# The first 40 microseconds of a two-layer transformer kernel: ScalarE normalisation, later constants, shared low parts, queries before keys

## The chip, the cores and the metric

The kernel is one program on one core of a Trainium2 chip. The metric is device time in microseconds for one launch that does everything: loading, both layers, storing.

The engines are TensorE (PE in the profile, with weight loads as PEld), VectorE (DVE), ScalarE (ACT), GpSimd (POOL) and SyncE (SP). Each runs its own instructions strictly in the order of its queue. DMAs are issued from the queues of SP, ACT and POOL.

## The reference

```python
x = L0_attn_hidden_states                      # (4, 512, 512)
x = x + layernorm(attn0(layernorm(x), Wq, Wkv, Wo))     # layer 0
x = x + layernorm(ffn0(layernorm(x), scales, vals, bias))
x = x + layernorm(attn1(layernorm(x), ...))             # layer 1
x = x + layernorm(ffn1(layernorm(x), ...))

def attn0(h, Wq, Wkv, Wo):                     # 32 query heads of 16, one key/value head of 16
    q = h @ Wq                                 # (4, 512, 512)
    k, v = split(h @ Wkv)                      # (4, 512, 16) each
    s = q . k * 16**-0.5 + alibi               # causal
    return (softmax(s) . v) @ Wo
```

Layer 1 has a low-rank attention with 32 heads of 128 and a ternary feed-forward part. The change touches only the layer-0 attention.

## The kernel before, in words

The work is in three stages that follow each other: `A1`/`A2` (layer 0, with layer 1's weight products mixed in, to about 680 us), `phase_b` (layer 1's attention) and `C` (layer 1's feed-forward part).

All products are made exact enough by splitting each float32 operand into a rounded high part and a low part, the difference (`split`, L66: ScalarE casts the high part at L68, another engine subtracts at L69). One product is then three matmuls: high by high (L160), high by low (L161), low by high (L162), in `mm3_gen`.

`A1.begin` (L543) is the start, and what the change touches:

- `ks_tile(i)` (L286) makes a key tile KS of batch i: a memset and two DMAs of 32 KB issued by GpSimd (L291). `qs_tile(m)` (L294) makes a query tile QS of head group m (8 heads) with two DMAs of 128 KB issued by GpSimd (L298). These constants carry the position bias.
- `load_x0` (L245) issues four DMAs from SP, one for each 128 rows of batch 0 (256 KB each, tile `ot`). `setup` (L259) loads the key weights from ScalarE's queue, and the four 256 KB pieces of the query weights and the mask from SP's. `setup_wq` (L273) splits the query weights in four pieces, with the subtraction on GpSimd.
- `front(b, x)` (L311) normalises the four row blocks of a batch (`ln_gen`, L99: statistics on VectorE, the power -0.5 on GpSimd at L108, the negative mean times scale on VectorE at L112). The normalised rows `xn` are made by ScalarE for batches 1 to 3 (L329) and by VectorE for batch 0 (`ln_apply`, L167). Then each block is transposed by TensorE (L148), its high part cast by ScalarE (L150, `xt_h`), its low part subtracted by VectorE (L152, `xt_l`). After the fourth block `front` projects keys and values (12 matmuls, into `po` for batch 0) and fills KS on ScalarE and VectorE (L352, L354).
- `qproj(b, m)` (L374) projects a group of queries (12 matmuls into `mm`), casts `qh` (L386), subtracts `ql` (L389), and for batch 0 calls `spread` (L400): for each of four pairs, two matmuls with a selection matrix (L409) and two ScalarE copies into QS (L412). Group 0 spreads through PSUM tiles `ps`, the other groups through the two `mm` banks that all projections share (`Tok(2)`).

After `begin`, `run` (L593) goes through 128 units and 13 more to drain. In unit u the row maxima of one column of scores are taken (`max_tile`: matmuls L453 and L457, a reduction on VectorE at L461). Twelve units later the exponentials (L496, L499) and the products with the values (L512) follow. Between these steps `slot` moves every generator in `gens` on by one step: the remaining projections (`projections`, L572), the reloads of queries (`loads`), and from unit 12 the weight products and the later parts of layer 0. Unit 8 m is the first that needs the queries of group m.

Program order is only a priority. `TileContext` orders each engine's queue before the launch, by its own modelled times; `issue_after(ins)` adds the rule that instructions traced in the block stand behind `ins` on the engine of `ins`.

Of the kernel before, what the change touches and what calls it, by code (L numbers as in the profile page):

```python
# [14 lines left out]
AF = mybir.ActivationFunctionType  # L15
# [27 lines left out]
def f(ap):  # L43
    return ap.bitcast(F32)
# [21 lines left out]
def split(nc, h, l, raw, eng):  # L66

    nc.scalar.copy(h, raw)  # L68
    return eng.tensor_tensor(l, raw, f(h), ALU.subtract)  # L69
# [29 lines left out]
def ln_gen(nc, c, pool, src, name="ln_nm"):  # L99

    st = pool.tile([128, 6], F32, name="ln_st", tag="ln_st")
    nc.vector.bn_stats(st, src)
    mv = pool.tile([128, 2], F32, name="ln_mv", tag="ln_mv")
    nc.vector.bn_aggr(mv, st)
    ve = pool.tile([128, 1], F32, name="ln_ve", tag="ln_ve")
    nc.vector.tensor_scalar(ve, mv[:, 1:2], 1e-5, None, ALU.add)
    rs = pool.tile([128, 1], F32, name="ln_rs", tag="ln_rs")
    c.last_pow = nc.gpsimd.tensor_tensor(rs, ve, c.mhalf, ALU.pow)  # L108
    yield from hop(3)
    nm = pool.tile([128, 1], F32, name=name, tag=name,  # L110
                   **({"bufs": 16} if name == "shift" else {}))
    nc.vector.scalar_tensor_tensor(nm, mv[:, 0:1], -1.0, rs, ALU.mult, ALU.mult)  # L112
    return rs, nm
# [31 lines left out]
def transpose_gen(nc, c, bank, src, dst_h, dst_l):  # L145
    ps = yield from bank.take([128, KC, 128])
    for k in range(KC):
        nc.tensor.transpose(ps[:, k, :], src[:, bass.ts(k, 128)], c.ident)  # L148
    yield from hop(1)
    nc.scalar.copy(dst_h, ps)  # L150
    yield from hop(2)
    nc.vector.tensor_tensor(dst_l, ps, f(dst_h), ALU.subtract)  # L152
    bank.give()
    yield from hop(1, 1)


def mm3_gen(nc, ps, lh, ll, rh, rl, ks, hops=2, stop=True):
    n = len(ks)
    for j, k in enumerate(ks):
        nc.tensor.matmul(ps, lh(k), rh(k), start=(j == 0), stop=False)  # L160
        nc.tensor.matmul(ps, lh(k), rl(k), start=False, stop=False)  # L161
        nc.tensor.matmul(ps, ll(k), rh(k), start=False, stop=(stop and j == n - 1))  # L162
        yield from hop(hops)


def ln_apply(nc, dst, src, rs, nm):
    nc.vector.tensor_scalar(dst, src, rs, nm, ALU.mult, ALU.add)  # L167
# [49 lines left out]
class A1:  # L217
# [54 lines left out]

    def setup_wq(self):  # L273
        for k in range(KC):
            last = split(self.nc, self.wq_h[:, k], self.wq_l[:, k], self.raw[:, k], self.nc.gpsimd)
        return last

    def setup_consts(self):
        with self.tc.issue_after(self.c.last_pow.ins):
            for m in range(1, 4):  # L280
                self.qs_tile(m)
            for i in range(1, B):
                self.ks_tile(i)
            self.zero = f(self.KS[B - 1][64:68, 0, :])
# [26 lines left out]
    def front(self, b, x):  # L311

        nc, c = self.nc, self.c
        mmp, tok = self.mmp, self.tok
        if x is None:
            x = {}
            for t in range(2):
                x[t] = self.load_x(b, t)
            yield from hop(8)
        while self.projected < 4 * b:  # L320
            yield
        xt_h = self.xtp.tile([128, KC, S], F32R, name="xt_h", tag="xt_h")
        xt_l = self.xtp.tile([128, KC, S], F32R, name="xt_l", tag="xt_l")
        self.xt = xt_h, xt_l
        for t in range(4):
            rs, nm = yield from ln_gen(nc, c, self.sm, x[t])
            xn = self.tmp.tile([128, D], F32, name="xn", tag="xn", bufs=3)
            if 1 and b > 0:
                nc.scalar.activation(xn, x[t], AF.Identity, bias=nm, scale=rs)  # L329
            else:  # L330
                ln_apply(nc, xn, x[t], rs, nm)
            if t + 2 not in x and t < 2:
                x[t + 2] = self.load_x(b, t + 2)
            yield from hop(2)
            ts = bass.ts(t, 128)
            yield from transpose_gen(nc, c, self.bank, xn, xt_h[:, :, ts], xt_l[:, :, ts])
        self.fronted = b + 1
        spare = b == 0
        if spare:
            ps = self.psO.tile([128, S], F32, name="po", tag="po")  # L340
        else:
            yield from tok.take()
            ps = mmp.tile([128, S], F32, name="mm", tag="mm")
        yield from mm3_gen(nc, ps, lambda k: self.wk_h[:, k], lambda k: self.wk_l[:, k],
                           lambda k: xt_h[:, k], lambda k: xt_l[:, k], range(KC))
        vt = self.qp.tile([32, S], F32, name="vt", tag="ql")
        nc.scalar.copy(vt, ps[32:64])
        yield
        for two in range(2):
            o = 64 * two  # L350
            ks = self.KS[b][:, two]
            nc.scalar.activation(ks[o:o + 48], ps[o:o + 48], AF.Copy, scale=0.25)  # L352
            yield from hop(3)
            nc.vector.scalar_tensor_tensor(  # L354
                ks[o + 32:o + 48], ps[o + 32:o + 48], 0.25, f(ks[o + 32:o + 48]),
                ALU.mult, ALU.subtract)
            yield
        if spare:
            psv = self.psT.tile([128, 4, 32], F32, name="ptv", tag="pt")
        else:  # L360
            tok.give()
            yield from tok.take()
            psv = mmp.tile([128, 4, 32], F32, name="mmv", tag="mm")
        for t in range(4):
            nc.tensor.transpose(psv[:, t], vt[:, bass.ts(t, 128)], c.ident[:32, :32])
        vx = self.vp.tile([128, 4, 32], F32, name="vx", tag="vx")
        nc.gpsimd.memset(vx, 1.0)
        yield
        nc.vector.tensor_copy(vx[:, :, 0:16], psv[:, :, 16:32])
        if not spare:  # L370
            tok.give()
        self.vx[b] = vx
# [170 lines left out]
    def begin(self):  # L543
        self.gens = []
        self.mn = None
        self.pe = {}
        self.tok = Tok(2)
        self.bank = Bank(self.mmp, "mm", self.tok)
        self.KS, self.QS = {}, {}
        self.ks_tile(0)  # L550
        self.qs_tile(0)
        x = self.load_x0()
        self.sel_tile()
        self.setup()
        fr = self.front(0, x)
        while True:
            n = self.c.__dict__.get("last_pow")
            next(fr)
            self.npow = getattr(self, "npow", 0) + (self.c.__dict__.get("last_pow") is not n)
            if self.npow == 4:  # L560
                break
        with self.tc.issue_after(self.c.last_pow.ins):
            last = self.setup_wq()
        with self.tc.issue_after(last.ins if 0 else self.c.last_pow.ins):
            self.setup_consts()
        for _ in fr:
            pass
        for m in range(2):
            for _ in self.qproj(0, m):
                pass  # L570

    def projections(self):  # L572

        for m in range(2, 4):
            yield from self.qproj(0, m)
        for b in range(1, B):
            yield from self.front(b, None)
            for m in range(4):
                yield from self.qproj(b, m)
# [814 lines left out]
```

## Time and profile before

| quantity | value |
|---|---|
| median of 3 runs | 2357.81 us (2349.78, 2357.81, 2358.64) |
| the profiled execution | 2349.14 us |
| its span, first to last instruction | 2347.1 us |
| TensorE busy | 2279.2 us (97%) |
| VectorE busy | 1577.6 us (67%) |
| ScalarE busy | 1069.2 us (46%) |
| GpSimd busy | 1175.6 us (50%) |
| mean granted TensorE clock | 0.999 |

The profiled execution took 2.04 us more than its span, and its time is that of the fastest of the three runs. TensorE is busy nearly everywhere except at the start, so the place to read is the first of the page's 40 slices and, inside it, what each engine waits for. A wait is named as waiter, then what released it.

### The profile page before, as it was taken

To read this page: it belongs to the slowest core of one execution; us is meant where nothing else is said; L and a number is where in the kernel's file an instruction comes from. 1 tells how busy PE (TensorE), PEld (TensorE's weight loads), DVE (VectorE), ACT (ScalarE), POOL (GpSimd) and SP (SyncE) were. 2 spreads that over 40 slices of the span, in tenths; PEclk is the share of its full clock that TensorE was granted. 3 is DMA by queue.
4 is the path that set the end of the run, shared out by engine and by line. 5 is a ranking of instruction groups with operands and counts; after the bars stand their busy time and mean duration, and the time that the engine had idled before them with its cause. 6 is when DMAs were issued, how large, how long until landed. Compare 5 with 4: busy or idle time off the path is not lost.

```text
span 2347.1 us, 35936 instructions
## 1 busy us (share of the span) xinstructions
PE 2279.2 (97%) x11638; PEld 1785.0 (76%) x11638; DVE 1577.6 (67%) x4664; ACT 1069.2 (46%) x2404; POOL 1175.6 (50%) x1390
## 2 busy tenths in 40 slices
PE   5999999999999999999999999999999999999998
PEld 4666566656677888888888888888888888878886
DVE  5755767676467777777777777777677678764443
ACT  4655555354424444444444444444444445443332
POOL 4323443434336656656656656666656657522221
PEclk9999999999999999999999999999999999999999
DMA  3555553534471412422422422412412312051100
GB/s 90 172 158 170 144 145 87 145 87 140 156 220 61 134 65 87 138 68 80 138 70 78 140 68 79 142 65 88 133 65 89 114 59 77 10 157 32 36 23 18
DMA packets 155534, 236.30 MB, mean 101 GB/s; under 512 B 26274, under 2 KB 91042, under 8 KB 146516
## 3 DMA queue, kind: packets, MB, share of 16 engines
q1 hardware_dynamic: 137732, 195.33, 26.8%
q0 software_dynamic: 14768, 35.92, 5.4%
q10 hardware_dynamic: 2848, 2.76, 0.4%
q8 instruction: 93, 1.52, 0.3%
q14 instruction: 93, 0.76, 0.1%
HBM read 180.03 MB, written 61.83 MB: 103 GB/s over the span
## 4 chain that ended last, share of the span: by engine, by line
PE 84%; DMA 4%; issue 4%; DVE 4%; ACT 2%; POOL 2%; SPq 0%; ACTq 0%; POOLq 0%; DVEq 0%
PE mm L183 11%; PE mm L184 10%; PE mm L185 10%; PE pt L978 5%; PE po L512 3%; PE mm L160 3%; PE mm L162 3%; PE mm L161 3%; PE po L992 3%; PE po L993 3%; PE po L991 3%; PE pt L496 3%; PE ps L958 3%; PE gu L1209 3%; PE ps L959 3%
## 5 line engine op out<-in xcount | busy, mean ns | idle before, releaser
L969 POOL TENSOR_TENSOR s<-s,r 128x384 f32<-128x384 f32 (+3 forms) x512 | 360.2, 721 | 122.6 <-DVE r L968 110.1
L966 ACT ACTIVATE s<-s,mn 128x384 f32<-128x384 f32 (+3 forms) x512 | 285.8, 560 | 226.6 <-DVE mn L962 225.0
L852 POOL TENSOR_TENSOR rp_a<-rp_a,rp_b 128x512 f32<-128x512 f32 x155 | 200.5, 1293 | 300.1 <-DVE rp_b L851 298.4
L981 ACT CAST ph<-pt 128x512 fp32r<-128x512 f32 x320 | 183.0, 586 | 306.5 <-PE pt L978 304.7
L461 DVE CUSTOM_DVE_ANT_0 jk<-ps,mask 128x384 bf16<-128x384 f32 (+3 forms) x512 | 227.2, 482 | 64.4 <-PE ps L457 63.3
L962 DVE CUSTOM_DVE_ANT_0 s<-ps,mask 128x384 f32<-128x384 f32 (+2 forms) x384 | 204.0, 552 | 41.0 <-PE ps L960 22.6
L982 DVE TENSOR_TENSOR pl<-pt,ph 128x512 fp32r<-128x512 f32 x320 | 218.1, 685 | 19.5 <-ACT ph L981 15.9
L499 ACT ACTIVATE pe<-pt 128x512 f32<-128x512 f32 x307 | 175.1, 601 | 96.0 <-PE pt L496 84.2
L183 PE MATMUL mm<-xh,w_h 128*128 128x512 f32 x512 | 206.3, 403 | 3.6 <-DVE rp_b L851 3.5
L978 PE MATMUL pt<-ident,s 128*128 128x128 f32 x1280 | 209.1, 272 | 0.3 <-DVE pl L982 0.2
L183 PE MATMUL mm<-w_h,oh 128*128 128x512 f32 x512 | 203.3, 397 | 2.6 <-DVE rp_b L851 1.9
L184 PE MATMUL mm<-xl,w_h 128*128 128x512 f32 x512 | 204.9, 400 | 0.0
L185 PE MATMUL mm<-xh,w_l 128*128 128x512 f32 x512 | 202.0, 395 | 0.0
L184 PE MATMUL mm<-w_l,oh 128*128 128x512 f32 x512 | 200.9, 392 | 0.0
L185 PE MATMUL mm<-w_h,ol 128*128 128x512 f32 x512 | 200.7, 392 | 0.0
L978 PEld LDWEIGHTS pt<-ident,s 128*128 128x128 f32 x1280 | 162.7, 140 | 44.2 <-POOL s L969 0.4
L501 POOL TENSOR_SCALAR_AFFINE_SELECT pe<-pe 128x512 f32<-128x512 f32 x128 | 83.2, 654 | 225.6 <-ACT pe L499 223.9
L854 POOL TENSOR_TENSOR ql<-rp_a,qh 128x512 fp32r<-128x512 f32 x124 | 160.2, 1292 | 20.4 <-ACT qh L853 20.1
L848 DVE TENSOR_TENSOR rp_a<-mm,cosq 128x512 f32<-128x512 f32 x128 | 88.3, 690 | 93.6 <-PE mm L185 84.0
L958 PE MATMUL ps<-k,qh 128*128 128x384 f32 (+2 forms) x384 | 139.1, 362 | 1.0 <-DVE mn L962 1.0
L998 DVE TENSOR_TENSOR ol<-po,oh 128x512 fp32r<-128x512 f32 x128 | 87.7, 685 | 68.9 <-ACT oh L997 68.8
L968 DVE RECIPROCAL r<-l 128x1 f32<-128x1 f32 x512 | 74.6, 157 | 87.8 <-ACT s L966 85.6
(330 smaller groups left out, 5796.8 us busy)
## 6 DMA issues: line engine op xcount, KB each, us to landing
xh<-xt SPq DMA_DIRECT2D x32, 1024.0 KB
xl<-xt SPq DMA_DIRECT2D x32, 1024.0 KB
raw<-in_a_wo SPq DMA_DIRECT2D x32, 256.0 KB
vh<-v SPq DMA_DIRECT2D x32, 256.0 KB
vl<-v SPq DMA_DIRECT2D x32, 256.0 KB
w_h<-in_a_wo POOLq DMA_DIRECT2D x32, 256.0 KB, 3.1
m_d<-t_d SPq DMA_DIRECT2D x192, 42.5 KB
raw<-in_a_wq SPq DMA_DIRECT2D x28, 256.0 KB
```

The lines of the kernel that those rows point to most:

```text
L183: nc.tensor.matmul(ps, lh(k), rh(k), start=(j == 0), stop=False)
L184: nc.tensor.matmul(ps, lh(k), rl(k), start=False, stop=False)
L185: nc.tensor.matmul(ps, ll(k), rh(k), start=False, stop=(j == n - 1))
L461: nc.vector.tensor_tensor_reduce(out=jk[:, :nk], in0=p, in1=self.c.mask[:, 384 - 128 * qb:512], scale=-1.0, scalar=3e38, op0=ALU.add, op1= ...
L852: eng.tensor_tensor(a, a, r, ALU.add)
L958: nc.tensor.matmul(ps[:, :nk], qh[:, qs], k[:, 0, :nk], start=True, stop=False)
L962: nc.vector.tensor_tensor_reduce(out=s[:, :nk], in0=ps[:, :nk], in1=mask, scale=-1.0, scalar=3e38, op0=ALU.add, op1=ALU.min, accum_out=mn)
L966: nc.scalar.activation(s[:, :nk], s[:, :nk], AF.Exp, bias=mn, scale=-1.0, accum_out=l)
L969: nc.gpsimd.tensor_tensor(s[:, :nk], s[:, :nk], r.to_broadcast([128, nk]), ALU.mult)
L978: nc.tensor.transpose(pt[:, j], PS[u, qb, j][:, bass.ts(kb, 128)], c.ident)
L981: nc.scalar.copy(ph, pt)
L982: nc.vector.tensor_tensor(pl, pt, f(ph), ALU.subtract)
```

## The change

Five edits, all at the start of layer 0:

1. `front` makes `xn` on ScalarE (L329) for batch 0 too; VectorE's `ln_apply` is no longer used there.
2. KS0 and QS0, with their four GpSimd DMAs, are made behind the fourth power of batch 0, no longer first of all.
3. `setup_wq` gives the low parts of pieces 0 and 1 to VectorE, those of 2 and 3 stay on GpSimd. The other constants (QS1 to QS3, KS1 to KS3) stand behind the last of these subtractions on GpSimd, before it was behind the fourth power.
4. `front` of batch 0 calls `qproj(0, 0)` ahead of its key and value projection.
5. `qproj(0, 1)` is no longer done in `begin`; it comes first in `projections`, inside `run`.

```diff
 def setup_wq(self):
     for k in range(KC):
-        last = split(self.nc, self.wq_h[:, k], self.wq_l[:, k], self.raw[:, k], self.nc.gpsimd)
+        last = split(self.nc, self.wq_h[:, k], self.wq_l[:, k], self.raw[:, k],
+                     self.nc.vector if k < 2 else self.nc.gpsimd)
     return last
 def setup_consts(self):
-    with self.tc.issue_after(self.c.last_pow.ins):
+    if True:
         for m in range(1, 4):
             self.qs_tile(m)
...
 def front(self, b, x):
...
-        if 1 and b > 0:
-            nc.scalar.activation(xn, x[t], AF.Identity, bias=nm, scale=rs)
-        else:
-            ln_apply(nc, xn, x[t], rs, nm)
+        nc.scalar.activation(xn, x[t], AF.Identity, bias=nm, scale=rs)
...
     spare = b == 0
+    if spare:
+        yield from self.qproj(0, 0)
     if spare:
         ps = self.psO.tile([128, S], F32, name="po", tag="po")
...
 def begin(self):
...
-    self.ks_tile(0)
-    self.qs_tile(0)
     x = self.load_x0()
...
     with self.tc.issue_after(self.c.last_pow.ins):
+        self.ks_tile(0)
+        self.qs_tile(0)
         last = self.setup_wq()
-    with self.tc.issue_after(last.ins if 0 else self.c.last_pow.ins):
+    with self.tc.issue_after(last.ins):
         self.setup_consts()
     for _ in fr:
         pass
-    for m in range(2):
+    for m in range(1, 1):
         for _ in self.qproj(0, m):
             pass
 def projections(self):
-    for m in range(2, 4):
+    for m in range(1, 4):
         yield from self.qproj(0, m)
```

## The prediction

> **What bounds the kernel now.** I read the page's 40 slices first, to find where TensorE is not full. Each digit is the busy share of a slice of 58.7 us in tenths.
>
> ```profile
> PE   5999999999999999999999999999999999999998
> ```
>
> Only the first slice has much to give. So the next view is the table of stretches, cut at what happens there: 23.2 us is the first projection matmul, 37.8 the first score, 66.1 the first exponential. Columns after the stretch: its length, then busy time (and instructions) of PE, PEld, DVE, ACT, POOL, then clock, DMA share, GB/s.
>
> ```profile
> 0.00:23.20 23.20, 4.14 (x16) 3.00 (x16) 15.21 (x34) 6.32 (x10) 18.43 (x35) 1.00 0.78 184
> 23.20:37.80 14.60, 13.80 (x52) 9.98 (x52) 5.50 (x14) 6.70 (x12) 4.67 (x10) 1.00 0.18 49
> 37.80:66.10 28.30, 23.47 (x94) 15.05 (x93) 20.45 (x97) 19.05 (x34) 1.12 (x3) 1.00 0.05 11
> 66.10:150.00 83.90, 79.07 (x428) 51.59 (x428) 57.29 (x216) 54.23 (x107) 28.86 (x36) 1.00 0.65 185
> ```
>
> TensorE idles 23.20 - 4.14 = 19.06 us before the projections, 0.80 us in them, 4.83 us between first score and first exponential: 24.69 us in all. Later it idles 4.83 us in 83.9 us, and it is busy for 97% of the span, so what is saved in the first 66 us arrives at the end nearly whole. 24.69 us is also the ceiling of any gain, 1.05% of the time.
>
> Third, the timeline of the first 24 us by engine, for what ends last there (start, duration, instruction). VectorE, then GpSimd:
>
> ```profile
> 11.94 0.55 DVE L167 TENSOR_SCALAR xn<-ot,ln_rs,ln_nm 128x512 f32<-128x512 f32 x1
> ...
> 14.43 2.23 DVE L167 TENSOR_SCALAR xn<-ot,ln_rs,ln_nm 128x512 f32<-128x512 f32 x1
> 16.58 1.22 DVE L112 SCALAR_TENSOR_TENSOR ln_nm<-ln_mv,ln_rs 128x1 f32<-128x1 f32 x1
> ...
> 18.33 1.85 DVE L167 TENSOR_SCALAR xn<-ot,ln_rs,ln_nm 128x512 f32<-128x512 f32 x1
> ```
>
> ```profile
> 14.45 1.95 POOL L298 DMA_DIRECT2D QS<-in_c_qs  x4
> 16.40 2.04 POOL L289 MEMSET KS<- 128x1024 f32 x2
> 18.42 2.88 POOL L69 TENSOR_TENSOR wq_l<-pe,wq_h 128x512 fp32r<-128x512 f32 x2
> ```
>
> The same instruction takes 0.55 us with GpSimd nearly free and 2.23 and 1.85 us while GpSimd issues DMAs, clears tiles and subtracts; the third ends (16.66) when the four DMA issues have ended (16.40). The chain of waits confirms that this is the path:
>
> ```profile
> 3.12 9.02 DMA pe<-in_a_wq
> 12.16 1.14 ACT wq_h L68 x2
> 13.82 0.69 DVE xt_l L152
> 14.51 2.15 DVE xn L167
> 16.66 1.14 DVE ln_nm L112
> 17.80 0.60 DVE ln_st L102
> 18.41 1.77 DVE xn L167
> 20.18 0.60 DVE ln_st L102
> 20.78 0.60 DVE xt_l L152
> 21.42 1.13 PE mm L148 x4
> ```
>
> From 14.51 to 21.38 the path lies on VectorE, 6.86 us. Before that it lies on the landing of the query weights, 9.02 us.
>
> **Edits 1 and 2, and the low parts: the first projection.** ScalarE's form of the row (L329) takes 0.82 us (0.80 to 0.83 over six). From the landing of the first weight piece ScalarE then has 4 casts of 0.62, 4 casts of 0.58 and 4 rows of 0.82: 8.1 us, from 11.08 to 19.2, if no row is done before: the projections start 4.0 us earlier than 23.21. The moved constants are 2 x 128 + 2 x 32 = 320 KB; at the 220 GB/s that all transfers made in the first 12 us, rows and weights land up to 1.5 us earlier: 17.7. The other bound is that the whole VectorE piece falls out, 6.86 us: 16.35. The power of row 0 (5.38) could make its row at 7, long before the weights, but its negative mean was queued until 11.12, so I do not count on this. I take 17.5, a gain of 5.7, between 3 and 6.9.
>
> KS0 and QS0 now issue behind the fourth power, which ended at 12.5. Their four issues take 2.2 us of GpSimd; the landing takes 2 to 7.6 us by the rows of their kind, so they are there by 22.5, and the first score needs them at about 30 (below). Price nothing; without that cover, at most the landing. They push the subtractions of pieces 2 and 3 (1.27 to 1.65 us each) to about 18; the matmul that first reads piece 2 is the ninth of its group, some 3 us after 17.5. Price 0, up to 1 us if the projections start at 16.4. Two subtractions move to VectorE, where the like (wk_l, from 5.47) takes 0.69 us; they replace 2.2 to 5.2 us of rows there. QS1 to QS3 and KS1 to KS3 (twelve issues of 0.49 us, three memsets of 0.94) run to about 27 on GpSimd. Behind them stand batch 1's powers, which ran at 23.37 and whose result was used at 31.24. Price 0.
>
> [...]
>
> **Edit 4: first score.** Before, 36 matmuls of three groups were interleaved and the first `qh` was cast 10.3 us after the first of them. With one group first, 12 matmuls at the pace of the chain (0.80, then five of 0.43, 0.36, then 0.23) take 4.5 us. The keys add 12 x 0.23 = 2.8, the eight selection matmuls 1.9: KS's chain can start 9.2 us after 17.5, at 26.7, and takes the 3.3 us that it took from 27.94 to 31.21. First score at 30.0, before 37.81. ScalarE has 8 copies of 0.58 and five other pieces in that time, about 8 us of 12.5, so it just covers. TensorE has 9.6 us of work (with 0.4 of transposes) in those 12.5: idle 2.9 instead of 0.80.
>
> **Edit 5: group 1 inside the loop.** It brings 12 matmuls and, of its eight selection matmuls, four that before ran ahead of 37.8: 16 x 0.23 = 3.7 us into the stretch that had 4.83 idle. VectorE is at 20.45 of 28.30 us there, ScalarE at 19.05: neither fills. I let the stretch keep its length, with idle 1.1. If it grows, the sharing of the two `mm` banks does it: groups 2 and 3 took some 11 us each from first matmul to last copy (44.63 to 56.10), and three of these need 33 us; by unit 8 only the first must be there. Growth 0 to 2 us.
>
> **Sum.** Idle before the first exponential: 17.5 - 4.15 = 13.35, 2.9 and 1.1, together 17.35, against 24.69: 7.3 us less; I take 7. The profiled execution took 2349.14 us (span 2347.1 and 2.04 around it), so it would come to 2342.1. Its time lies 8.67 us below the median, at the lowest of the three runs, which spread over 8.86 us. Carried to the median: 2357.81 - 7 = 2350.8, forecast 2350.
>
> **Rivals.** *More than the start.* The path between score and exponential also holds two landings of batch 1's rows, 4.01 and 4.39 us (`DMA x<-in_x` in the chain), for which VectorE's queue stood 2.2 us once. If the new queue order is free of both, some 7 us more: 2343.8. For it: those waits come from the queue order alone. Against: the two tiles for x and their release by ScalarE stay.
>
> *The written order does not decide.* The queues are ordered by modelled times; before, query and key matmuls already interleaved (`po` at 23.21, `mm` at 23.80, `po` at 24.23). If they do so again, or the loop's stretch grows by 2 us and more, only the first term is left, about 4: 2354.
>
> *Slower: batch rows wait for ScalarE.* In VectorE's queue the statistics of a batch's third and fourth block stand ahead of maxima; their rows load only when ScalarE has made an earlier `xn`. SP's waits in the first 75 us show the dependence (waiter, releaser, us in total, times, longest):
>
> ```profile
> SPq L256 <- ACT xn L329: 49.7, 5, 22.9
> ```
>
> The change adds group 1's copies (eight of 0.58) inside the loop, ahead of that on ScalarE. One such stand cost VectorE 2.17 us. Batches 1 to 3 have 12 blocks: with 9 stands (19.5 us, less the 7 gained) the loss passes 0.5%; with 12 it is 19 us, 2377. Against it: only one stand of this size is in the first 75 us, and VectorE has a third of its time free.
>
> **How the numbers follow.** A measurement of this kernel can tell about 0.5% from no change: below 2346.0 is faster, above 2369.6 slower. Forecast 0.43, of which 0.17 falls below 2346.0, because 4 us separate them and the runs spread over 8.9. More than the start 0.22 (0.20 faster). Written order 0.20 (0.04 faster). Slower 0.15 (0.13 past the bound). Together faster 0.41, same 0.46, slower 0.13. The range goes from 2335, the larger gain at the lower end of the runs' spread (2349.78 - 14), to 2364, no gain and 6 us lost.
>
> **What would show it.** Right: no L167 in the first 24 us, `xn` at 0.82 on ACT; first projection at 16.4 to 19.2; first score near 30, first exponential near 58; idle of TensorE up to there near 17 us. [...]

## The result and the profile after

| | before | after |
|---|---|---|
| median of 5 runs each, same chip | 2353.54 us (2349.78 to 2358.64) | 2338.62 us (2333.68 to 2341.16) |
| ratio | | 0.9932 [0.9918, 0.9946] |
| the profiled execution | 2349.14 us | 2340.92 us |
| its span | 2347.1 us | 2339.2 us |
| mean granted TensorE clock in it | 0.999 | 0.994 |

The changed kernel is faster by 14.9 us in the medians (0.63% of 2353.54; the ratio says 0.68%); on a second chip the ratio was 0.9945 [0.9932, 0.9959], 12.7 us. The two profiled executions lie only 8.2 us apart, and the last row of the table is part of why: the profile of before is an uncommonly undisturbed one (runs of it beside the experiments have clocks of 0.993 to 0.998).

TensorE's row of the 40 slices in the changed kernel: the first digit has gone from 5 to 7, no other digit moved.

```profile
PE   7999999999999999999999999999999999999998
```

The table of stretches, cut at the same events as before: first projection, first score, the first matmul of an exponential (L496; at 66.1 before, at 57.2 now), and 83.9 us behind that (columns as before: length, then PE, PEld, DVE, ACT, POOL, clock, DMA share, GB/s).

```profile
0.00:15.50 15.50, 4.46 (x16) 2.87 (x16) 10.44 (x31) 9.23 (x14) 10.77 (x25) 1.00 0.69 224
15.50:29.80 14.30, 13.49 (x52) 10.15 (x53) 4.83 (x11) 6.71 (x13) 9.20 (x17) 1.00 0.64 105
29.80:57.20 27.40, 24.06 (x92) 16.02 (x93) 20.87 (x99) 19.07 (x34) 1.66 (x3) 0.94 0.06 14
57.20:141.10 83.90, 80.00 (x443) 52.86 (x441) 60.79 (x230) 54.29 (x107) 30.66 (x37) 1.00 0.68 198
```

The three events came 7.7, 8.0 and 8.9 us earlier. TensorE idles 11.04, 0.81 and 3.34 us in the three stretches, 15.2 us in all where it was 24.69; the clock of 0.94 in the third comes from 3.41 us at 0.50 (32.15 to 35.56).

The timeline of the first 17 us, nine rows of ScalarE, VectorE and GpSimd out of the whole (start, duration, instruction):

```profile
5.36 0.69 DVE L69 TENSOR_TENSOR wk_l<-pe,wk_h 128x512 fp32r<-128x512 f32 x1 [0.43 <-ACT wk_h L68]
6.75 0.81 ACT L329 ACTIVATE xn<-ot,ln_nm,ln_rs 128x512 f32<-128x512 f32 x1 [1.42 <-DVE ln_nm L112]
7.47 1.24 ACT L68 CAST wq_h<-pe 128x512 fp32r<-128x512 f32 x2
8.17 2.31 POOL L108 TENSOR_TENSOR ln_rs<-ln_ve,mhalf 128x1 f32<-128x1 f32 x3 [2.60 <-DVE ln_ve L106]
9.38 0.69 DVE L69 TENSOR_TENSOR wq_l<-pe,wq_h 128x512 fp32r<-128x512 f32 x1
10.44 1.25 POOL L292 DMA_DIRECT2D KS<-in_c_ks  x2
10.99 1.52 ACT L329 ACTIVATE xn<-ot,ln_nm,ln_rs 128x512 f32<-128x512 f32 x2
11.67 0.97 POOL L299 DMA_DIRECT2D QS<-in_c_qs  x2
12.65 2.50 POOL L69 TENSOR_TENSOR wq_l<-pe,wq_h 128x512 fp32r<-128x512 f32 x2
```

The rows of `xn` are all on ScalarE, the first at 6.75, ahead of the first cast of query weights (7.47). Before, that cast had to wait for the landing until 11.08:

```profile
11.08 0.62 ACT L68 CAST wq_h<-pe 128x512 fp32r<-128x512 f32 x1 [5.64 <-DMA pe<-in_a_wq]
```

GpSimd issues KS0 and QS0 behind the powers and subtracts behind these. The chain of waits, its longer steps, shows what ends last now:

```profile
0.80 3.89 DMA pe<-in_a_wk
4.71 0.63 ACT wk_h L68
5.36 0.69 DVE wk_l L69
6.05 0.60 DVE ln_st L102
6.75 0.82 ACT xn L329
7.61 1.13 PE mm L148 x4
8.77 0.59 ACT xt_h L150
9.38 0.69 DVE wq_l L69
10.15 0.60 DVE xt_l L152
11.09 1.42 ACT xn L329 x2
...
15.55 0.79 PE mm L160
...
36.60 2.65 DMA x<-in_x
57.85 6.02 DMA x<-in_x
```

The 9.02 us landing of the query weights has left the path; the key weights' landing of 3.89 us stands first. The piece of 6.86 us on VectorE has become single steps that take turns with ScalarE. Two landings of batch 1's rows are still there, 2.65 and 6.02 us; the second starts behind the first exponential. SyncE's wait on ScalarE's rows, which the slower rival lived on, did not grow (49.7 us before; first 75 us; waiter, releaser, us in total, times, longest):

```profile
SPq L256 <- ACT xn L329: 47.7, 6, 20.8
```

One thing has not moved: group 1. The change takes its projection out of `begin`, yet TensorE still runs it ahead of the first score, directly behind the keys (first and last of its twelve matmuls):

```profile
22.56 0.39 PE L160 MATMUL mm<-xt_h,wq_h 128*128 128x512 f32 x1
...
25.76 0.39 PE L162 MATMUL mm<-xt_h,wq_l 128*128 128x512 f32 x1
```

Counted in the traces from event to event, 24 query matmuls and 12 selection matmuls precede the first score in both kernels, and 92 matmuls lie between it and the first exponential's in both.

### The profile page after: what moved, and what is told of

Read it like the earlier page. It is cut to its first block, busy times and chain, and to the rows that moved or that the text cites. A ratio compares the mean times of both kernels' runs of the same rounds, so it can differ in the third digit from the quotient of the medians.

```text
span 2339.2 us, 35933 instructions
## 1 busy us (share of the span) xinstructions
PE 2280.7 (97%) x11638; PEld 1789.4 (76%) x11638; DVE 1575.2 (67%) x4662; ACT 1072.4 (46%) x2408; POOL 1175.7 (50%) x1388
## 4 chain that ended last, share of the span: by engine, by line
PE 83%; DMA 5%; issue 4%; DVE 4%; ACT 2%; POOL 1%; SPq 0%; ACTq 0%; POOLq 0%; DVEq 0%
PE mm L183 11%; PE mm L184 10%; PE mm L185 10%; PE pt L978 5%; PE mm L160 3%; PE po L512 3%; PE mm L162 3%; PE mm L161 3%; PE po L992 3%; PE po L993 3%; PE po L991 3%; PE ps L958 3%; PE gu L1209 3%; PE ps L959 3%; PE ps L960 3%
## 5 line engine op out<-in xcount | busy, mean ns | idle before, releaser
L982 DVE TENSOR_TENSOR pl<-pt,ph 128x512 fp32r<-128x512 f32 x320 | 218.0, 686 | 19.7 <-ACT ph L981 16.4
L962 DVE CUSTOM_DVE_ANT_0 s<-ps,mask 128x384 f32<-128x384 f32 (+2 forms) x384 | 204.1, 552 | 39.4 <-PE ps L960 22.5
L499 ACT ACTIVATE pe<-pt 128x512 f32<-128x512 f32 x307 | 175.3, 601 | 93.0 <-PE pt L496 84.0
L854 POOL TENSOR_TENSOR ql<-rp_a,qh 128x512 fp32r<-128x512 f32 x124 | 160.4, 1294 | 23.3 <-ACT qh L853 23.3
L108 POOL TENSOR_TENSOR ln_rs<-ln_ve,mhalf 128x1 f32<-128x1 f32 x112 | 63.9, 578 | 145.4 <-DVE ln_ve L106 127.3
```

What stands on the lines that cost most here:

```text
L962: nc.vector.tensor_tensor_reduce(out=s[:, :nk], in0=ps[:, :nk], in1=mask, scale=-1.0, scalar=3e38, op0=ALU.add, op1=ALU.min, accum_out=mn)
L982: nc.vector.tensor_tensor(pl, pt, f(ph), ALU.subtract)
```

## The experiments

All times are compared with runs of the kernel before on the same chip, made beside them. The landmarks are from one profile each, in us; the first exponential is here ScalarE's (L499), half a microsecond behind its matmul:

| kernel | first projection | first score | first exponential | first score of layer 1 | span | median, ratio |
|---|---|---|---|---|---|---|
| before | 23.2 | 37.8 | 66.6 | 684.8 | 2347.1 | |
| after | 15.6 | 29.8 | 57.7 | 673.8 | 2339.2 | 0.9932 |
| `only_xn` | 18.9 | 33.5 | 62.7 | 680.4 | 2340.8 | 0.9973 |
| `only_g1` | 23.3 | 38.5 | 66.1 | 675.3 | 2334.3 | 0.9947 |
| `undo_xn` | 17.6 | 32.3 | 61.5 | 672.3 | 2333.7 | 0.9958 |
| `undo_g1` | 15.6 | 31.1 | 58.9 | 681.1 | 2337.9 | 0.9950 |
| `undo_const` | 19.7 | 34.7 | 62.1 | 675.8 | 2336.1 | single run |
| `undo_wl` | 15.6 | 29.9 | 59.5 | 676.4 | 2340.0 | single run |
| `undo_later` | 15.9 | 35.9 | 64.4 | 681.5 | 2344.1 | single run |
| `undo_qk` | 15.7 | 31.1 | 60.6 | 673.0 | 2335.8 | single run |
| `before_order` | 22.5 | 38.3 | 67.4 | 676.9 | 2333.4 | 0.9924 |

The first question: is it only the start that is shorter (theory A), or did edit 5 also change the order of TensorE's queue in the loop and shorten it (theory B)?

**Edit 1 alone** (`only_xn`). Before, with

```diff
-            if 1 and b > 0:
-                nc.scalar.activation(xn, x[t], AF.Identity, bias=nm, scale=rs)
-            else:
-                ln_apply(nc, xn, x[t], rs, nm)
+            nc.scalar.activation(xn, x[t], AF.Identity, bias=nm, scale=rs)
```

> The kernel before with edit 1 alone: batch 0's rows made by ScalarE. TensorE's queue is that of before in all but 10 places among the first 55 matmuls, so this is a test of the start by itself. Theory A (what the start gains is carried to the end, nothing else matters): the 6.9 us that the path spent on VectorE from 14.5 to 21.4 falls to some 2 us, first projection near 18.5 instead of 23.2, and the time falls by the same 4 to 6 us, to a ratio of 0.9975 to 0.998. Theory B (half of the measured gain comes from another order in the loop of layer 0): the same here. Rival C (a gain at the start is taken back by later waits): ratio 0.9995 to 1.0005, with the first projection early all the same.

Measured: 2344.36 us against 2350.53, ratio 0.9973 [0.9962, 0.9984], 6.2 us. The first projection came 4.4 us earlier, the first exponential 3.9, the end of the span 6.3. TensorE's queue is that of before but for 10 places. So what the start saves arrives at the end, as the prediction held: rival C falls, since even the upper end of the interval is below its 0.9995.

**Edit 5 alone** (`only_g1`). Before, with

```diff
-        for m in range(2):
+        for m in range(1):
             for _ in self.qproj(0, m):
...
-        for m in range(2, 4):
+        for m in range(1, 4):
             yield from self.qproj(0, m)
```

> The kernel before with edit 5 alone: query group 1 projected inside the loop. The start keeps its order (TensorE's queue differs from matmul 178 on), the loop of layer 0 gets nearly the order of the changed kernel. Theory A (the start carries all): first projection at 23.2 and first score at 37.8 as before, ratio 0.999 to 1.001. Theory B (the order in the loop is worth half of the gain, some 7 us): same start, ratio 0.9965 to 0.9975, the difference arising between the first exponential and the first score of layer 1.

Measured: 2338.63 us against 2350.53, ratio 0.9947 [0.9935, 0.9959], 11.9 us, with a start as long as before (23.29, 38.47, 66.07). Theory A falls: a kernel whose first 66 us are as long as before gained most of what the whole change gained, and more than theory B had put on it. From first exponential to first score of layer 1 it took 609.2 us, before 618.2. Matched in order by their tiles, 171 of the first 3500 matmuls of its queue stand elsewhere than in after, 1373 elsewhere than in before.

**The change without edit 1** (`undo_xn`) and **without edit 5** (`undo_g1`).

```diff
-            nc.scalar.activation(xn, x[t], AF.Identity, bias=nm, scale=rs)
+            if 1 and b > 0:
+                nc.scalar.activation(xn, x[t], AF.Identity, bias=nm, scale=rs)
+            else:
+                ln_apply(nc, xn, x[t], rs, nm)
```

> The changed kernel with batch 0's rows on VectorE again. The loop keeps the changed kernel's order (226 of 11125 matmuls stand elsewhere, all among the first 484). Theory A: the start loses what edit 1 gave, 4 to 6 us; against the kernel before 0.9950 to 0.9960 by the medians (0.9932 for the whole change). If the other edits at the start give most (constants behind the rows land the rows and weights earlier), the loss is under 2 us: 0.9932 to 0.994. Theory B says the same as A here, since the loop's order stays.

Measured: 2340.47 us, ratio 0.9958 [0.9944, 0.9971], inside the range that A and B share, so it does not separate them. The first projection came 2.0 us later than in after, the first score 2.5, the first exponential 3.75. With the constants out of the way VectorE's rows are short until GpSimd issues KS0 and QS0, from 10.67 to 12.86 (timeline of `undo_xn`, three of the four rows):

```profile
7.22 0.52 DVE L167 TENSOR_SCALAR xn<-ot,ln_rs,ln_nm 128x512 f32<-128x512 f32 x1
10.50 0.54 DVE L167 TENSOR_SCALAR xn<-ot,ln_rs,ln_nm 128x512 f32<-128x512 f32 x1
11.03 1.61 DVE L167 TENSOR_SCALAR xn<-ot,ln_rs,ln_nm 128x512 f32<-128x512 f32 x1
```

So edit 1 is worth 4.4 us at the first projection when it comes first and 2.0 when it comes last: part of what it cures, the stretched rows, the moved constants cure too.

```diff
-        for m in range(1, 1):
+        for m in range(1, 2):
             for _ in self.qproj(0, m):
...
-        for m in range(1, 4):
+        for m in range(2, 4):
             yield from self.qproj(0, m)
```

> The changed kernel with query group 1 projected ahead of the loop again. The start keeps its times (TensorE's queue differs from matmul 174 on), the loop's order differs. Theory A: ratio 0.9925 to 0.994, as the whole change, first projection near 15.5 and first exponential near 57.7. Theory B: only the start's 8 us remain, ratio 0.9960 to 0.9970.

Measured: 2339.64 us, ratio 0.9950 [0.9939, 0.9962], between the two ranges. The start kept all but 1.2 us; from first exponential to first score of layer 1 it took 622.2 us, after 616.1. That is theory B's sign, but the gain, 10.9 us, is only 1.8 to 4.0 us below that of after. Layer 1, which the edit does not touch, took part of it back: from its first output projection on it took 1624.1 us, in after 1629.5 (more on this at `before_order`). The effects of edits 1 and 5 do not add either (6.2 + 11.9 = 18.1 us alone, 12.7 to 14.9 together with the rest).

**What the other edits do to the start**: one execution each, so read by landmarks and not by time. KS0 and QS0 first again (`undo_const`):

```diff
+        self.ks_tile(0)
+        self.qs_tile(0)
         x = self.load_x0()
...
-            self.ks_tile(0)
-            self.qs_tile(0)
             last = self.setup_wq()
```

> The changed kernel with KS0 and QS0 made first of all again. Theory D (the four constant transfers, 320 KB, stand ahead of rows and weights): the first projection moves from 15.5 to 17 us, the last row's statistics start 1 to 1.5 us later than 7.3. Rival (edit 1 alone sets the start, transfers are hidden): first projection within 0.4 us of 15.5.

Measured: first projection at 19.68, 4.1 us later. Theory D had the sign and was too small. ScalarE's timeline in `undo_const` shows why: the query weights' first cast waits for its landing until 10.09 (7.47 in after), and three casts in a row then keep the rows waiting.

```profile
10.09 0.62 ACT L68 CAST wq_h<-pe 128x512 fp32r<-128x512 f32 x1 [4.82 <-DMA pe<-in_a_wq]
10.62 0.81 ACT L329 ACTIVATE xn<-ot,ln_nm,ln_rs 128x512 f32<-128x512 f32 x1
11.34 1.78 ACT L68 CAST wq_h<-pe 128x512 fp32r<-128x512 f32 x3
```

All low parts on GpSimd again (`undo_wl`):

```diff
-            last = split(self.nc, self.wq_h[:, k], self.wq_l[:, k], self.raw[:, k],
-                         self.nc.vector if k < 2 else self.nc.gpsimd)
+            last = split(self.nc, self.wq_h[:, k], self.wq_l[:, k], self.raw[:, k], self.nc.gpsimd)
```

> The changed kernel with all four low parts of the query weights on GpSimd. Four subtractions of 1.3 us behind the four constant issues end near 18 instead of 15.1. If the later pieces still have cover (the third is first read some 2 us after the first projection), first projection 15.5 and first score 29.8 to 30.5. If VectorE's two low parts held up its other work, the start comes earlier without them: first projection near 14.9.

Measured: first projection 15.58, first score 29.86, both those of after within 0.1 us. Sharing the low parts is worth nothing here; GpSimd does all four between 11.95 and 16.9, ahead of their use. The first query cast came at 23.68 and not at 20.20, since keys stand ahead of group 0's last matmuls in this queue, and the first score is no later for it. (The first exponential came 1.8 us later; this profile has 6.8 us at half clock from 33 us on, after has 3.4 from 32.)

The other constants behind the fourth power again (`undo_later`):

```diff
-        if True:
+        with self.tc.issue_after(self.c.last_pow.ins):
             for m in range(1, 4):
...
-        with self.tc.issue_after(last.ins):
+        with self.tc.issue_after(last.ins if 0 else self.c.last_pow.ins):
             self.setup_consts()
```

> The changed kernel with the other constants (QS1 to QS3, KS1 to KS3) again behind the fourth power, not behind the last low part. If their six 0.49 us issues go ahead of the last two low parts, these end near 18 and the first group's matmuls on pieces 2 and 3 wait up to 1 us: first score 30 to 31. Rival: nothing waits for them, first projection 15.5, first score 29.8.

Measured: first projection +0.4 us, but first score +6.1 and first exponential +6.7. The expectation missed. GpSimd's timeline in `undo_later`, and ScalarE's first query cast:

```profile
11.60 3.87 POOL L299 DMA_DIRECT2D QS<-in_c_qs  x8
15.40 2.81 POOL L290 MEMSET KS<- 128x1024 f32 x3
18.10 2.57 POOL L69 TENSOR_TENSOR wq_l<-pe,wq_h 128x512 fp32r<-128x512 f32 x2
26.22 0.58 ACT L386 CAST qh<-mm 128x512 fp32r<-128x512 f32 x1 [10.37 <-PE mm L162]
```

Eight issues (two of them QS0's, which stand there in after too) and three memsets stand ahead of the subtractions of pieces 2 and 3, and the first query cast is at 26.22 where after has it at 20.20. TensorE does not wait for these subtractions: it is busy without a pause from 15.91 to 26.4, and its queue has the matmuls on pieces 2 and 3 behind the keys and group 1. Then the second half of KS on ScalarE stands behind eight copies, at 34.46 (24.70 in after), and the first score behind that. In this arrangement the words "behind the last subtraction" are worth 6 us at the first score, by way of the order of the queues.

Keys and values ahead of queries again (`undo_qk`):

```diff
-        if spare:
-            yield from self.qproj(0, 0)
...
-        for m in range(1, 1):
+        for m in range(1):
             for _ in self.qproj(0, m):
```

> The changed kernel with query group 0 projected behind keys and values again (TensorE's queue differs in 35 of its first 62 matmuls and nowhere else). Theory E (queries first save the selection and copy chain): first projection 15.5, the first query cast 2 to 3 us later than 20.2, first score 32 to 33. Rival F (ScalarE's copies and the key chain take the same time in either order): first score within 0.7 us of 29.8.

Measured: first query cast +4.0 us, first score 31.09 (+1.3), first exponential 60.63 (+2.9). That lies between the two theories: the written order of queries and keys does decide, for less at the first score than E put on it.

**What in the loop's order costs time.** The trace shows one thing that differs between the orders. A product with the values (L512) is four matmuls on four column groups of the array, which the trace counts as two each, so a whole product is "x8". Queued together they take as long as one of them alone. TensorE's timeline in before has a product of 128 columns broken into three pieces, two single matmuls and a pair (start, duration, instruction):

```profile
202.43 0.41 PE L512 MATMUL po<-pe,vx 128*32 128x128 f32 x2
202.76 0.50 PE L496 MATMUL pt<-QS,KS 128*128 128x512 f32 x1
...
203.61 0.41 PE L512 MATMUL po<-pe,vx 128*32 128x128 f32 x2
203.94 0.28 PE L469 MATMUL ps<-ident,mn 128*32 128x128 f32 x1
204.16 0.41 PE L512 MATMUL po<-pe,vx 128*32 128x128 f32 x4
204.50 0.50 PE L162 MATMUL mm<-xt_h,wq_l 128*128 128x512 f32 x1
```

From the start of each piece to the next start it is 0.33, 0.33 and 0.34 us, 1.00 together. A whole one of the same size, here in `before_order`, takes 200.85 - 200.49 = 0.36:

```profile
200.49 0.43 PE L512 MATMUL po<-pe,vx 128*32 128x128 f32 x8
200.85 0.28 PE L469 MATMUL ps<-ident,mn 128*32 128x128 f32 x1
```

It is the same at the other sizes: a lone matmul and a whole product (median) take 0.55 and 0.57 us at 256 columns, 0.76 and 0.78 at 384, 0.98 and 1.00 at 512. Summed over the loop (first exponential to first score of layer 1, start to next start, waits taken off); the last two rows are estimates, with the time at half clock counted at half (in after, projection matmuls follow each other at 0.43 us at 683 us, at half clock, and at 0.23 us at 675 us):

| | before | `undo_g1` | after | `only_g1` | `before_order` |
|---|---|---|---|---|---|
| products broken off singly | 14 | 17 | 7 | 6 | 0 |
| queue time of products, us | 92.5 | 97.4 | 91.0 | 87.9 | 85.8 |
| the loop, us | 618.2 | 622.2 | 616.1 | 609.2 | 609.6 |
| of it at half clock, us | 0 | 13.7 | 10.2 | 3.4 | 13.7 |
| products at full clock, us | 92.5 | 93.4 | 88.5 | 87.9 | 84.4 |
| the loop at full clock, us | 618.2 | 615.4 | 611.0 | 607.5 | 602.7 |

The loops do not hold quite the same work: in `undo_g1` and `before_order` twelve matmuls of one product (`wv`, 2.8 us) stand behind the first score of layer 1 that the others have ahead of it. With these, `undo_g1`'s loop at full clock is as long as that of before (618.2), and 7.2 us longer than that of after, which is the size that theory B gave to edit 5.

Theory P: broken products are what the order costs. **Two kernels to force them whole** (`before_whole`, `after_whole`) put the four matmuls into a critical section:

```diff
-        for hh in range(4):
+        with self.tc.tile_critical():
+          for hh in range(4):
             nc.tensor.matmul(po[32 * hh:32 * hh + 32, 128 * kb:512], self.vx[b][:, kb, :],
```

> The kernel before, with each group of four matmuls of the values product (L512, one per column group) kept together in TensorE's queue. In the kernel before 128 groups stand in 128 stretches of very uneven length, among them 14 single matmuls; here all 128 are whole. Theory P (a matmul broken off its group takes as long as the whole group, and that is most of what edit 5 saved in the loop): the time that TensorE's queue spends on these products falls from 92.5 to 86 us, ratio 0.9965 to 0.9975, start unchanged. Rival Q (edit 5's gain came from fewer waits for VectorE): ratio 0.999 to 1.001, though the products do take less.

> The changed kernel with the four matmuls of each values product kept together. Theory P: 7 single matmuls and 7 broken pairs or triples go, the products fall from 91 to 86 us, ratio to the kernel before 0.991 to 0.9925 (0.9932 for the changed kernel). Rival Q: 0.9925 to 0.994. If the new order of the loop happens to add waits, 0.994 and more.

Measured: 2590.43 us, ratio 1.1028 [1.1013, 1.1043], and 2591.45 us, 1.1026 [1.101, 1.1041]. The test is spoilt and says nothing on P: in it TensorE stands ahead of the groups until other engines and DMAs are through (waits of TensorE in `before_whole`: waiter, releaser, us in total, times, longest).

```profile
PE po L513 <- ACT pe L499: 19.5, 30, 1.3
PE po L513 <- DVE mn L461: 17.7, 18, 1.8
PE po L513 <- issue: 16.7, 16, 2.9
PE po L513 <- DMA QS<-qh_d: 14.3, 5, 4.4
```

**The changed kernel on that chip** (`after_again`) was run beside them for the ratio.

> The changed kernel once more on the chip of the two others, so that they can be compared with it: 0.992 to 0.9945. Its runs should differ among themselves by the number of 3.4 us stretches at half clock (five such in the first profile), about 1.7 us of time each.

Measured: 2337.42 us against 2350.11, ratio 0.9945 [0.9932, 0.9959].

**Before with another order and nothing else** (`before_order`): the priority of the products in the written program, not their work, is changed, which leaves no product broken.

```diff
-                    with prio(self.tc, 0):
+                    with prio(self.tc, 300):
                         self.pv(v - 2)
                         self.pv(v - 1)
```

> The kernel before with only the priority of the values products (L512) raised for the ordering (prio offset 300 instead of 0). All 128 groups of four come out whole in TensorE's queue, with no waits added by a critical section; 1435 of the first 3500 matmuls stand elsewhere, as many as edit 5 moves (1417). The start keeps its order. Theory P (a broken-off matmul takes as long as its whole group): the queue time of these products falls from 92.5 to 86 us and the time with it, ratio 0.9965 to 0.9975. Rival Q (waits for VectorE and ScalarE in the loop decide): the products fall to 86 us, but idle time in the loop moves by as much or more, and the ratio is anywhere from 0.996 to 1.004, following the idle time.

Measured: 2334.18 us (2331.16 to 2335.62) against 2350.46, ratio 0.9924 [0.9911, 0.9937], 16.3 us. The start is that of before (22.5, 38.3, 67.4). Products take 85.8 us, as P said (86), TensorE's idle time in the loop 20.8 us where it was 23.2. One number in the kernel before is worth as much as all five edits, by the ratios. But the gain is more than twice what P allowed for (0.9965 to 0.9975), and Q's range does not hold it either: the products and the idle time account for 6.7 + 2.4 = 9.1 of the 16.3 us. With half clock counted at half the products give 8.1 and idle time 2.4 of the 15.5 us that the loop lost, and 2.8 are the twelve matmuls that left it.

Layer 1 is shorter as well, 1656.5 us from its first score to the end instead of 1662.3, although it has taken in those twelve matmuls. TensorE idles 15.2 us in it where it was 20.0 (before, then `before_order`, columns as above):

```profile
684.80:2347.10 1662.30, 1642.33 (x8177) 1359.22 (x8175) 1130.36 (x3032) 725.12 (x1768) 922.48 (x1014) 1.00 0.26 83
676.90:2333.40 1656.50, 1641.28 (x8189) 1361.10 (x8187) 1134.64 (x3033) 723.67 (x1769) 927.88 (x1020) 1.00 0.25 85
```

The edit does not touch that stage, but the reordering reaches it: from there on TensorE's queue has another matmul than before's in 4279 places, and it is, matmul for matmul, the queue of `undo_g1`. These two kernels took 1624.1 us from layer 1's first output projection on, ten others 1627.0 to 1630.1. That the order of layer 1 makes the difference fits this, but no run changes it alone. Whether the changed kernel gains as much from the same number was not run.

## Why the prediction was right or wrong

The time fell inside the range, 3.6 us above its low end. The forecast was "no change that can be measured" by a narrow margin over "faster"; it is faster, and the gain of 12.7 to 14.9 us is about twice the 7 of the sum. The range held it by luck: its low end was set by a rival whose mechanism did not occur, and the loop, which gave the rest, was in no term.

- *First projection* (17.5, bounds 16.4 to 19.2): 15.55, 2 us better than the value and outside the bounds. The right mechanism, a mis-sized term: the earlier landing was put at up to 1.5 us, but the query weights' first cast came 3.6 us earlier (11.08 to 7.47), and `undo_const` gives 4.1 us at the projection to the place of KS0 and QS0. The assumption that no row is done ahead of the weights did not hold either: row 0's negative mean came at 6.57 (11.12 before), as it stood behind two blocks' statistics and no longer behind four (in before VectorE idled 1.85 us up to 8.94, for the third block's landing, though this mean's power had ended at 5.95), and the row at 6.75, a case that the working had named and not counted on.
- *Rows on ScalarE*: 0.81 us in place of up to 2.23, as costed; 4.4 us alone, 2.0 on top of the rest.
- *Low parts and other constants, price 0*: the low parts are free (`undo_wl`), and so is the final arrangement. But the clause that puts QS1 to KS3 behind the subtractions was costed only for what waits behind it. Without it the first score is 6.1 us later (`undo_later`). What a step keeps out of the way is a price too.
- *Subtractions on VectorE*: the two `wq_l` took 0.69 us each at 8.17 and 9.38, beside GpSimd's three powers (8.17 to 10.48), as long as `wk_l` (0.69 at 5.36). What took longer was GpSimd: its powers took 1.10, 0.54 and 0.72 us, where `undo_wl`, with no `wq_l` on VectorE, has 0.55 for each. No subtraction of GpSimd's ran beside them (12.65 to 15.1), so how long such a pair takes side by side is not tested.
- *Queries first* (first score 30.0): 29.80, but that is luck, two errors that cancel. From first projection to first score the sum had 12.5 us, before it was 14.6; it took 14.25. The first query cast came 4.65 us after the first projection, predicted 4.5. What failed is the step behind it: group 1, meant for the loop, ran at 22.6 to 26.2, ahead of the first score, so that TensorE idled 0.81 us there and not 2.9. To that extent the rival "the written order does not decide" was true, and `undo_qk` gives edit 4 1.3 us at the first score, where the sum shortened this stretch by 2.1.
- *Group 1's sixteen matmuls come into the stretch from score to exponential* (3.7 us): none did, the stretch has the 92 that it had. It took 27.4 us, predicted 28.3, although 3.4 us of it ran at half clock; its matmul of the first exponential came at 57.2, predicted near 58. Idle up to there 15.2 us, predicted 17.35.
- *The start's gain arrives at the end*: so in `only_xn` (3.9 us at the first exponential, 6.2 by the median, 3.8 to 8.9 by its interval). The 7 us of the sum became 8.9.
- *What was missing*: the loop. The prediction priced edit 5 by its sixteen matmuls in one stretch of 28 us. These did not move; what moved are some 1400 of the first 3500 matmuls of TensorE's queue against each other, and `only_g1` is 11.9 us faster with an unchanged start. Of the 9.0 us that its loop lost, 4.6 are the products, 3.5 idle time, 1.5 the exponentials' matmuls (L496), with 0.6 lost elsewhere. In the pair of profiles shown, the loop's gain hides: the profile of after has three stretches of 3.4 us at half clock in the loop and before none. At half the work in each, an estimate from these rows, that is 5 us that the medians do not show (clocks of 0.994 to 0.996 in the runs of after, 0.993 to 0.998 in those of before beside the experiments).
- *"More than the start"*: the size was right (14 predicted, 12.7 to 14.9 measured), the mechanism wrong. Both landings of batch 1's rows are still in the chain. The working misread them, too: only the first lay between score and exponential, the one of 4.39 us starts at 66.75, behind the exponential.
- *The slower rival* did not occur: SyncE's waits on ScalarE are 47.7 us, before 49.7.

What stays open: how much of the order's gain is broken products. `before_order` shows that order alone moves this kernel by 16 us; the products' 6.7 us (8.1 at full clock) are seen in the trace, the rest, layer 1's part in it, is not settled.

## What to carry to other kernels

Where a scheduler orders the queues, an edit at one place can reorder hundreds of instructions elsewhere, and that can weigh more than what the edit was costed for: run the part that reorders alone, and look at the stretch far from the edit. Here the four matmuls of a product, on four column groups, took 0.36 us at 128 columns when they stood next to each other in the queue, and each piece of a broken product took 0.33 or 0.34, so look for lone ones. Of a step with a rule of order, cost what the rule keeps out of the way as well as what stands behind it, and compare medians, not one profile, where stretches at half clock move single executions, here by the 5 us estimated above.

## What the runs showed of the hardware

TensorE's clock fell to half at the end of both profiles shown: 0.50 in the last 6.56 us of before and in the last 6.47 of after, with no matmul in them. Ahead of that it fell in after for 3.41 us each at 32, 250, 496 and 554 us and for 6.83 at 681; in before it was 1.00 from 26 to 2340.5 us. The other profiles have mean clocks of 0.994 to 0.998 (0.994 in `undo_wl`, with seven stretches of 3.4 us, two of them back to back), the two kernels with critical sections 0.957 and 0.956. In after, around 32 us (stretches, columns as above):

```profile
28.00:32.00 4.00, 2.43 (x9) 1.47 (x9) 2.85 (x14) 3.89 (x7) 0.65 (x2) 1.00 0.29 87
33.00:34.00 1.00, 1.00 (x5) 0.91 (x5) 0.40 (x4) 0.96 (x3) 0.00 (x0) 0.50 0.00 0
36.00:37.00 1.00, 1.00 (x6) 0.83 (x5) 1.00 (x7) 0.98 (x2) 0.00 (x0) 1.00 0.00 0
```

TensorE was busy for 61% of the 4 us before (2.43 of 4.00), its longest single wait 0.7 us; then it is full and at 0.50, and from 36 us it has 1.00 again. In the last 3.41 us ahead of the stretches at 32, 250, 496 and 554 us it was busy for 58, 32, 26 and 40%, with no wait over 2.6 us; ahead of that at 681 us it did not work at all, in a wait of 4.8 us. So the clock fell behind partly busy stretches as well as behind a long wait, and what sets it off is not shown by these runs.

VectorE's rows took longer beside GpSimd's issues, for KS0 and QS0 as for other tiles. In `undo_xn` a row took 0.52 us at 7.22 with GpSimd idle and 1.61 at 11.03 beside the issues of KS0 and QS0 (0.54 at 10.50; the issues began at 10.67); in before 0.55 at 11.94 and 2.23 at 14.43, the longer one beside four issues for the other QS tiles.
